# Element-wise work moved from GpSimd to VectorE, and two norms moved behind their products, in a fused convolution, scan, attention and expert kernel

## The chip, the cores and the metric

The kernel runs on one core of a Trainium2 chip. The metric is the time of one execution on the device in microseconds (us). Three timed runs of the kernel before gave 5311.55, 5321.8 and 5326.36 us; the median is 5321.8 us.

A core has TensorE (PE in the profile; PEld is its weight load), VectorE (DVE), ScalarE (ACT), GpSimd (POOL) and SyncE (SP), which here issues the transfers. Each engine works through its own instructions in the order in which the program put them.

## The reference, cut to what matters

The input is four images of 128 channels and 64 x 64 pixels, all float32. Layer 0 is a group norm, then

```
xn  = ln(x);  y = xn + fc2(gelu(ln(conv3x3(xn))))
chunks = ln(y), split in 4 groups of 32 channels
m   = mamba(chunks) + skip * chunks          # scan over the 4096 pixels
out = ln(xn + m) @ proj_w.T + proj_b;  x = x + out
```

In the scan, `delta = softplus(...)`, the state is multiplied by `exp(delta * A)` and driven by `delta * B * xin` (16 states for each of 64 inner channels), and the read-out is gated: `y * silu(z)`. Layer 1 works on the pixels as tokens t:

```
t = t + softmax(q k^T / sqrt(128)) v @ W_proj + b_proj   # q, k, v from ln(t); 4 heads of 32
probs = softmax(ln(t) @ router_w + router_b)             # 8 experts, the best 2, their shares made to sum to 1
t = t + sum over the 2 of share * (ln(t) @ expert_w + expert_b)
```

## The kernel before

The 4096 pixels of an image are 8 blocks of 512 columns (`BLK`). A main loop at the end of the kernel runs in **slots**. Its scan has 512 units (4 images x 8 blocks x 2 halves of the channels x 8 pairs of states) of two slots each, so 1024 slots (`END`). In each slot the loop puts, by hand and in a fixed order, one step of everything on the engines: `tensor`, `vector`, `scalar`, `gpsimd` and `sync` are wrappers (`queued`, L445) that chain each instruction to the previous one of its engine. Nearly all instructions therefore carry line 445, and are told apart by the names of their tiles.

- **Scan.** In a unit ACT makes the decays `da` (`decayed`, L747), DVE multiplies the broadcast rows by `du` (`driven`, L767, tile `h`), runs the scan (`scan`, L772) and multiplies by the read-out rows (`read`, L781, tile `hc`); PE turns and sums `hc` into `y`. ACT also copies the last states (`kept`, L762, tile `state`).
- **Attention.** `attention` (L940) yields one group a slot: 2 tiles of 128 keys against 1024 queries of a head. PE makes the scores `sc`, ACT their exponentials `pT` (`exponentials`, L1001), and PE adds the weighted values into `av` a slot later (`weighted`, L1009). An image has 256 groups. Its keys are taken in 10 runs (`RUNS`, L931) as blocks become ready (`ready`, L936). At the end of a run ACT copies `av` to `avs`, and where an earlier run of the same queries exists (96 of 160), GpSimd adds its sum `prev`.
- **Lanes.** The rest is cut into small steps by `yield`, in two lanes that advance twice a slot each (`advance`, L1186). Lane X does a step at the end of a slot and the next at the start of the following slot; lane Y does its two in the middle. Lane Y: group norm, first norm, `conv` (L611; by PE for the first image, by 9 multiply-adds on DVE for the others) and `inputs` (L681), which prepares a half block for the scan; its softplus correction and `du` are five GpSimd operations (L723 to L727). Lane X: `closed` (L816) ends layer 0 for a block and makes keys, queries and values, and `finished` (L1059) does projection, router and experts. After END lane Y runs `finished` too.
- **Norms.** `normalised` (L504) takes statistics on DVE, a power and a product on GpSimd (`rs`, `shift`), and after two yields four ACT operations (`xt`). In lane X it is used twice in `closed` (on `cm`, then on `tt`) and once in `finished` (on `acc`).
- **`held`** (L532) keeps `inputs` and the first norm of `closed` from using lane X's one PSUM tile at the same time; one waits two steps at a time while the other has it.
- In `finished`, PE also adds the residual: after the expert bias product it multiplies `acc` by the identity into the same PSUM tile, and ACT copies the sum to `res`. Eight expert products follow, with `share` rows fetched from memory.

Of the kernel before, what the change touches and what calls it, by code (L numbers as in the profile page):

```python
# [9 lines left out]
F32 = mybir.dt.float32  # L10
# [7 lines left out]
P = 128  # L18
# [18 lines left out]
def conv_mamba_attn_moe_kernel(ctx: ExitStack, tc: tile.TileContext, t: dict):  # L37
# [65 lines left out]
    with (  # L103
        tc.tile_pool(name="bound", bufs=1) as bd,
        tc.tile_pool(name="ps_w", bufs=2, space=PSUM) as ps_w,
    ):
        pw = ps_w.tile([P, P], F32, name="pw")
        nc.tensor.matmul(pw, lhsT=xdt, rhs=dtT, start=True, stop=True)
        nc.vector.tensor_copy(wdt, pw)
        pw = ps_w.tile([P, P], F32, name="pw")  # L110
        nc.tensor.matmul(pw[0:1, :], lhsT=bvc, rhs=wp, start=True, stop=True)
        crow1 = bd.tile([1, C], F32, name="crow1")
        nc.vector.tensor_add(crow1, pw[0:1, :], bp)
        pw = ps_w.tile([P, P], F32, name="pw")
        nc.tensor.matmul(pw, lhsT=ones, rhs=crow1, start=True, stop=True)
        nc.vector.tensor_copy(crow, pw)

        sq = bd.tile([P, 2 * NH + 1], F32, name="sq")
        nc.vector.memset(sq, 0.0)
        bsq = bd.tile([DH, 2 * NH], F32, name="bsq")
        for i, (w, bias) in enumerate(((wqn, bqn), (wkn, bkn))):
            for h in range(NH):
                r = slice(DH * h, DH * h + DH)
                pw = ps_w.tile([P, P], F32, name="pw")
                nc.tensor.matmul(pw[0:DH, 0:DH], lhsT=w[:, r], rhs=w[:, r], start=True, stop=True)
                g = bd.tile([DH, DH], F32, name="g", bufs=2)
# [24 lines left out]
        nc.gpsimd.memset(power[:, 2 * NH :], 0.5)  # L154
        wn = bd.tile([1, 2 * NH], F32, name="wn")
        nc.gpsimd.tensor_tensor(wn, norm[:, 0 : 2 * NH], power[:, 0 : 2 * NH], ALU.pow)
        nc.gpsimd.tensor_tensor(bnorm, bnorm, power[:, 2 * NH :], ALU.pow)
        most = bd.tile([1, 2 * NH], F32, name="most")
        nc.vector.scalar_tensor_tensor(most, wn, 1.001 * float(C) ** 0.5, bnorm, ALU.mult, ALU.add)
        score = bd.tile([1, NH], F32, name="score")  # L160
        nc.vector.tensor_mul(score, most[:, 0:NH], most[:, NH:])
        fine = bd.tile([1, NH + 1], F32, name="fine")
        nc.vector.tensor_scalar(fine[:, 0:NH], score, SCORE_MAX / ATT_SCALE, None, ALU.is_le)
        nc.vector.tensor_scalar(
            fine[:, NH : NH + 1], norm[:, 2 * NH : 2 * NH + 1], VALUE_MAX, None, ALU.is_le
        )
        ok = bd.tile([1, 1], F32, name="ok")
        nc.vector.tensor_reduce(ok, fine, AX.X, ALU.min)
        nc.vector.tensor_scalar(ok, ok, -1.0, 1.0, ALU.mult, ALU.add)
        nc.vector.tensor_copy(general, ok)  # L170
    setup.close()


# [277 lines left out]
    def mm(out, lhsT, rhs, start=True, stop=True):  # L451
        tensor.matmul(out, lhsT=lhsT, rhs=rhs, start=start, stop=stop)
# [42 lines left out]
    def transposed(lane, src):  # L495
        ps = work(lane)
        for j in range(NT):
            tensor.transpose(ps[:, j * P : (j + 1) * P], src[:, j, :], ident)
        return ps

    def by_tile(src):
        return src.rearrange("p (j c) -> p j c", c=P)

    def normalised(lane, src):  # L504


        st = small.tile([P, NT, 6], F32, name=f"st{lane}")
        mv = small.tile([P, NT, 2], F32, name=f"mv{lane}")
# [3 lines left out]
            vector.bn_aggr(out=mv[:, j, :], in_=st[:, j, :])  # L512
        rs = small.tile([P, NT], F32, name=f"rs{lane}")
        vector.tensor_scalar_add(rs, mv[:, :, 1], EPS)
        shift = small.tile([P, NT], F32, name=f"shift{lane}")
        vector.tensor_scalar_mul(shift, mv[:, :, 0], -1.0)
        gpsimd.tensor_tensor(rs, rs, mhalf, ALU.pow)
# [163 lines left out]
    def inputs(b, i, p):  # L681
# [38 lines left out]

        du = mix.tile([P, BLK], F32, name="du", bufs=2)
        lost = du
        gpsimd.tensor_scalar(lost, e, 1.0, -1.0, ALU.add, ALU.add)  # L723
        gpsimd.tensor_sub(lost, e, lost)
        gpsimd.tensor_add(ln, ln, lost)
        gpsimd.tensor_add(delta, delta, ln)
        gpsimd.tensor_mul(du, delta, xin)  # L727
        in_of[b, i, p] = xin, zs, delta, du, bcd
        done.add(("in", b, i, p))
        yield  # L730
# [55 lines left out]
    def scanned(b, i, p, y):  # L786
        xin, zs, delta, du, bcd = in_of.pop((b, i, p))
        vector.scalar_tensor_tensor(xin, xin, dsk, y, ALU.mult, ALU.add)
        gpsimd.tensor_mul(zs, xin, zs)
        gated[b, i, p] = zs  # L790

    def turned_on(y, term, first, last):
# [23 lines left out]
    def closed(b, i):  # L816
# [23 lines left out]
        done.add(("freed", b, i))  # L840
        yield
        vector.tensor_add(cm, ps, cm)
        gpsimd.tensor_add(by_tile(xr), by_tile(xr), projb[:, None, :].to_broadcast([P, NT, C]))
        yield
        while held:
            yield
            yield
        held.add("closed")
        ps = transposed("X", by_tile(cm))
        yield  # L850
        xt = yield from normalised("X", by_tile(ps))
        held.clear()
        ps = transposed("X", xt)
        yield
        f = tmp("X", "f")
        scalar.activation(f, ps, AF.Identity, bias=lnb, scale=lnw)
        yield
        ps = work("X", [P, NT, C])
        for j in range(NT):
            mm(ps[:, j, :], f[:, j * P : (j + 1) * P], projT)  # L860
        yield
        tt = side.tile([P, NT, C], F32, name="tt")
        vector.tensor_add(tt, ps, by_tile(xr))
        send(tsave[b][:, s], tt.rearrange("p j c -> p (j c)"), 2)
        xt = yield from normalised("X", tt)

        tr = tmp("X", "tr", [P, NT, C])
        gpsimd.tensor_add(tr, tt, crow[:, None, :].to_broadcast([P, NT, C]))
        send(td[:, s], tr.rearrange("p j c -> p (j c)"), 2)
        ps = transposed("X", xt)  # L870
        yield
# [137 lines left out]
    def weighted(group):  # L1009
# [9 lines left out]
                )  # L1019
        if last:  # L1020
            avs = att.tile([P, BLK], F32, name="avs", bufs=2)
            scalar.copy(avs, av)
            if prev is not None:
                gpsimd.tensor_add(avs, avs, prev)


            if not final:
# [31 lines left out]
    def finished(b, qb, lane):  # L1059
# [18 lines left out]
            mm(ps[:, j, :], aT[:, j * P : (j + 1) * P], wp)  # L1078
        yield
        vector.tensor_add(acc, ps, acc)  # L1080
        xt = yield from normalised(lane, acc)
        ps = transposed(lane, xt)
        yield
        xf = tmp(lane, "xf")
        scalar.copy(xf, ps)
# [8 lines left out]

        yield

        pr = routed("pr")
        vector.tensor_add(pr, ps, rb[:, None, :].to_broadcast(wide))
        m = routed("m", 1)
        vector.tensor_reduce(m, pr, AX.X, ALU.max)  # L1100
        vector.tensor_sub(pr, pr, m.to_broadcast(wide))
# [22 lines left out]
        vector.tensor_mul(pr, pr, pick1)  # L1124
        vector.tensor_add(top1, top1, top2)
        vector.reciprocal(top1, top1)
        vector.tensor_mul(pr, pr, top1.to_broadcast(wide))
        yield

        ps = work(lane)  # L1130
        for j in range(NT):
            tensor.transpose(ps[0:NE, j * P : (j + 1) * P], pr[:, j, :], ident)
        yield
        prT = tmp(lane, "prT")[0:NE, :]
        scalar.copy(prT, ps[0:NE, :])
        shares = dram.tile([NE, BLK], F32, name=f"shares{lane}")
        send(shares, prT)
        yield

        def share(e):  # L1140
# [10 lines left out]


        ps = work(lane)
        mm(ps, eb8, prT, True, False)
        for j in range(NT):
            mm(ps[:, j * P : (j + 1) * P], acc[:, j, :], ident, False, j == NT - 1)
        yield
        res = tmp(lane, "res")
        scalar.copy(res, ps)
        yield  # L1160
        ahead = deque(share(e) for e in (0, 2))
        yield
# [106 lines left out]
    units = [(b, i, p, n) for b, i in blocks for p in range(2) for n in range(0, NST, 2)]  # L1269
    END = 2 * len(units)  # L1270

    ALONE = NB // 2 * NST
    rows, due, closing, y_of = {}, deque(), deque(), {}
    h_of, slot = {}, 0

# [182 lines left out]
```

## Time and profile before

| quantity | value |
|---|---|
| median of the timed runs | 5321.8 us |
| profiled execution, its own time | 5310.32 us |
| its span, first to last instruction | 5308.5 us |
| mean granted TensorE clock | 0.956 |
| ACT `pT` / `da` / table loads | 1986.7 / 747.5 / 409.3 us |
| DVE scan `h` x512 | 1256.1 us, 2453 ns each |
| DMA queue 1 | 62.8% of 16 engines' span |

The profile is of one execution. Busy time is what an engine spent inside instructions; idle time of an engine is put down to the instruction that released it. The execution's own time exceeds its span by 1.8 us.

### The profile page before, as it was taken

The page shows a single profiled execution, that of the slowest core. Times are in us where ns is not written, and L with a number is a line of the kernel's source. Part 1 is how long each engine was busy: PE and PEld are TensorE (multiplying, and loading weights), DVE is VectorE, ACT ScalarE, POOL GpSimd, SP SyncE. Part 2 cuts the span into 40 slices and gives each one's busy share as a digit, 9 for nine tenths or more (in the row PEclk, how much of TensorE's full clock was granted, in tenths as well). Part 3 has the DMA queues.
Part 4 walks back from the last instruction along what each step waited for, and adds up shares of the span by engine and source line. Part 5 has one row for each costly group of instructions (what it writes and reads, how often), then busy time and mean ns, then how long its engine had stood idle before and what let it go on. Part 6 is the DMA issues. An engine that isn't in the chain of part 4 may idle for free. (4 is left out here: it accounts for less than half of the span.)

```text
span 5308.5 us, 64113 instructions
## 1 busy us (share of the span) xinstructions
PE 4795.3 (90%) x21066; PEld 2336.3 (44%) x21066; DVE 3691.3 (70%) x5123; ACT 3916.8 (74%) x6117; POOL 1441.9 (27%) x1091
## 2 busy tenths in 40 slices
PE   4556898999999999899999999999999999999997
PEld 2333444444444444444444444444444444443443
DVE  4888767777777877877777877877777877740322
ACT  3455787888888787688888888788888887756553
POOL 2333224333322223223322223323422223201000
PEclk8777999999999999899999999999999999999998
DMA  3555666666766666667766666767766666744532
GB/s 96 182 181 190 211 213 232 234 221 236 250 222 218 237 209 237 223 226 256 252 231 224 230 217 228 262 223 252 250 237 227 227 221 220 261 160 156 178 132 68
DMA packets 451702, 1131.71 MB, mean 213 GB/s; under 512 B 51985, under 2 KB 135330, under 8 KB 451362
## 3 DMA queue, kind: packets, MB, share of 16 engines
q1 hardware_dynamic: 450194, 1126.74, 62.8%
q8 instruction: 169, 2.77, 0.2%
q14 instruction: 171, 1.40, 0.1%
q10 hardware_dynamic: 1168, 0.80, 0.0%
HBM read 967.12 MB, written 143.39 MB: 209 GB/s over the span
## 5 line engine op out<-in xcount | busy, mean ns | idle before, releaser
L445 ACT ACTIVATE pT<-sc 128x1024 f32<-128x1024 f32 x2048 | 1986.7, 1025 | 757.9 <-PE sc L445 755.5
L445 PE MATMUL av<-pT,v 128*64 128x512 f32 x8192 | 1997.8, 609 | 9.0 <-ACT avs L445 8.8
L445 PE MATMUL sc<-qs,ks 128*128 128x512 f32 x4096 | 1305.5, 437 | 96.9 <-DMA ks<-kd 48.3
L445 DVE TENSOR_TENSOR_SCAN h<-da,state,h 128x1025 f32<-128x1025 f32 x512 | 1256.1, 2453 | 131.7 <-ACT h L445 108.1
L445 PEld LDWEIGHTS sc<-qs,ks 128*128 128x128 f32 x4096 | 700.9, 190 | 799.1 <-ACT pT L445 322.6
L445 PEld LDWEIGHTS av<-pT,v 128*64 128x64 f32 x8192 | 499.7, 137 | 838.8 <-issue 808.2
L445 ACT ACTIVATE da<-delta,amat 128x512 f32<-128x512 f32 x1024 | 747.5, 734 | 5.9 <-POOL delta L445 4.0
L445 DVE TENSOR_TENSOR h<-rows,du 128x1024 f32<-128x1024 f32 x512 | 702.7, 1372 | 66.5 <-POOL du L445 25.8
L445 DVE TENSOR_TENSOR hc<-rows,h 128x1024 f32<-128x1024 f32 x512 | 677.3, 1323 | 33.9 <-PE y L445 13.9
L445 PE MATMUL y<-ident,hc 128*128 128x128 f32 x4096 | 622.4, 283 | 64.7 <-DVE hc L445 64.7
L445 PEld LDWEIGHTS y<-ident,hc 128*128 128x128 f32 x4096 | 516.8, 146 | 235.3 <-issue 88.0
L445 POOL TENSOR_TENSOR rsY<-rsY,mhalf 128x4 f32<-128x4 f32 x100 | 148.8, 1488 | 1377.0 <-DVE shiftY L445 1377.0
L445 ACT ACT_TABLE_LOAD x319 | 409.3, 1283 | 22.2 <-PE ps_Y L445 17.1
L445 POOL TENSOR_TENSOR zs<-xin,zs 128x512 f32<-128x512 f32 x64 | 141.3, 2207 | 808.3 <-DVE xin L445 779.6
L445 POOL TENSOR_TENSOR rsX<-rsX,mhalf 128x4 f32<-128x4 f32 x92 | 199.9, 2172 | 537.8 <-DVE shiftX L445 537.4
L445 POOL TENSOR_TENSOR avs<-avs,prev 128x512 f32<-128x512 f32 x96 | 152.4, 1588 | 642.4 <-ACT avs L445 556.9
L445 ACT ACTIVATE xt<-ps_Y,shiftY,rsY 128x128 f32<-128x128 f32 x380 | 143.6, 469 | 112.7 <-POOL shiftY L445 105.7
L445 PE MATMUL ps_X<-share,w_ew 128*128 128x512 f32 x432 | 214.4, 619 | 0.0
L445 POOL TENSOR_SCALAR du<-e 128x512 f32<-128x512 f32 x64 | 127.5, 1992 | 289.0 <-ACT e L445 289.0
L445 DVE TENSOR_TENSOR share<-share,xf 128x1024 f32<-128x1024 f32 x128 | 156.8, 1225 | 47.7 <-DMA share<-sharesY 32.0
L445 DVE RECIPROCAL den<-den 128x32 f32<-128x32 f32 x16 | 5.5, 346 | 220.0 <-DMA den<-total 219.9
L445 ACT COPY avs<-av 128x512 f32<-128x512 f32 x160 | 95.2, 595 | 81.2 <-PE av L445 66.2
(238 smaller groups left out, 4394.2 us busy)
## 6 DMA issues: line engine op xcount, KB each, us to landing
rows<-bcd SPq DMA_DIRECT2D x1024, 512.0 KB
ks<-kd SPq DMA_DIRECT2D x192, 512.0 KB
qs<-qd SPq DMA_DIRECT2D x161, 512.0 KB
share<-sharesX SPq DMA_DIRECT2D x108, 512.0 KB
v<-vd SPq DMA_DIRECT2D x192, 256.0 KB
ks<-kd SPq DMA_DIRECT2D x128, 256.0 KB
avd<-avs SPq DMA_DIRECT2D x96, 256.0 KB
prev<-avd SPq DMA_DIRECT2D x96, 256.0 KB
```

Of the source, the lines that this page charges most:

```text
L445: return lambda *args, **kw: queued(op(*args, **kw))
```

## The change

**GpSimd to VectorE.** The five softplus operations of `inputs`, the gate product in `scanned` (L786), the two row additions in `closed` (`projb` into `xr`, `crow` into `tr`) and the addition of `prev` at the end of an attention run are issued on DVE. The last reads `av` from PSUM itself, so ACT copies `av` only where there is no `prev`. GpSimd keeps the powers (and the small products and copies beside them).

**Norms behind products.** The mean is taken out of the weights: at the start, `rw`, each expert's matrix and `projT` (with `lnw` in it, and `lnb` folded into `projb`) are multiplied by `ident - 1/128` (`centred`). In `closed` the first norm gives way to `spread` (statistics and power only): `cm` is multiplied by `projT` as it is, and `rs` multiplies the product as it is added to `xr`. In `finished` the raw `acc` is turned, `rs` multiplies the router's logits, and a second copy of the shares, multiplied by `rs`, goes to the experts. The residual is added by DVE from the turned `acc` (`xf`), not by PE. `closed` has four yields fewer and no longer looks at `held`; `finished` has two fewer. The second norm of `closed` and the norms of lane Y stay.

```diff
+        cen = bd.tile([P, P], F32, name="cen")
+        nc.vector.tensor_scalar(cen, ident, 1.0 / C, None, ALU.subtract)
+        def centred(w, src):
+            n = w.shape[1]
+            for k in range(0, n, P):
+                pw = ps_w.tile([P, P], F32, name="pw")
+                m = min(P, n - k)
+                nc.tensor.matmul(pw[:, 0:m], lhsT=cen, rhs=src[:, k : k + m], start=True, stop=True)
+                nc.vector.tensor_copy(w[:, k : k + m], pw[:, 0:m])
+        centred(rw, rw)
...
+        centred(ewf, ewf)
...
+        centred(projT, gain)
...
+    def spread(lane, src):
+        mv, rs = moments(lane, src)
+        gpsimd.tensor_tensor(rs, rs, mhalf, ALU.pow)
+        return rs
...
-        gpsimd.tensor_scalar(lost, e, 1.0, -1.0, ALU.add, ALU.add)
-        gpsimd.tensor_sub(lost, e, lost)
-        gpsimd.tensor_add(ln, ln, lost)
-        gpsimd.tensor_add(delta, delta, ln)
-        gpsimd.tensor_mul(du, delta, xin)
+        vector.tensor_scalar(lost, e, 1.0, -1.0, ALU.add, ALU.add)
+        vector.tensor_sub(lost, e, lost)
+        vector.tensor_add(ln, ln, lost)
+        vector.tensor_add(delta, delta, ln)
+        vector.tensor_mul(du, delta, xin)
...
-        gpsimd.tensor_mul(zs, xin, zs)
+        vector.tensor_mul(zs, xin, zs)
...
-        while held:
-            yield
-            yield
-        held.add("closed")
         ps = transposed("X", by_tile(cm))
         yield
-        xt = yield from normalised("X", by_tile(ps))
-        held.clear()
-        ps = transposed("X", xt)
-        yield
-        f = tmp("X", "f")
-        scalar.activation(f, ps, AF.Identity, bias=lnb, scale=lnw)
+        rs = spread("X", by_tile(ps))
         yield
         ps = work("X", [P, NT, C])
         for j in range(NT):
-            mm(ps[:, j, :], f[:, j * P : (j + 1) * P], projT)
+            mm(ps[:, j, :], cm[:, j * P : (j + 1) * P], projT)
         yield
         tt = side.tile([P, NT, C], F32, name="tt")
-        vector.tensor_add(tt, ps, by_tile(xr))
+        for j in range(NT):
+            vector.scalar_tensor_tensor(
+                tt[:, j, :], ps[:, j, :], rs[:, j : j + 1], xr[:, j * P : (j + 1) * P],
+                ALU.mult, ALU.add,
+            )
...
-            scalar.copy(avs, av)
-            if prev is not None:
-                gpsimd.tensor_add(avs, avs, prev)
+            if prev is None:
+                scalar.copy(avs, av)
+            else:
+                vector.tensor_add(avs, av, prev)
...
-        xt = yield from normalised(lane, acc)
-        ps = transposed(lane, xt)
+        rs = spread(lane, acc)
+        yield
+        ps = transposed(lane, acc)
...
-        vector.tensor_add(pr, ps, rb[:, None, :].to_broadcast(wide))
+        vector.tensor_mul(pr, ps, rs[:, :, None].to_broadcast(wide))
+        vector.tensor_add(pr, pr, rb[:, None, :].to_broadcast(wide))
...
-        vector.tensor_mul(pr, pr, top1.to_broadcast(wide))
+        vector.tensor_mul(both[:, :, 0:NE], pr, top1.to_broadcast(wide))
+        vector.tensor_mul(both[:, :, NE:], both[:, :, 0:NE], rs[:, :, None].to_broadcast(wide))
...
-        mm(ps, eb8, prT, True, False)
-        for j in range(NT):
-            mm(ps[:, j * P : (j + 1) * P], acc[:, j, :], ident, False, j == NT - 1)
+        mm(ps, eb8, prT[0:NE, :])
         yield
         res = tmp(lane, "res")
-        scalar.copy(res, ps)
+        vector.tensor_add(res, ps, xf)
```

More of the change, by code (lines that the diff above doesn't have):

```diff
@@ L170, in conv_mamba_attn_moe_kernel @@
         nc.vector.tensor_copy(general, ok)
+        cen = bd.tile([P, P], F32, name="cen")
[8 more added lines that the diff above has]
+        centred(rw, rw)
+        ewf = ew.rearrange("p e c -> p (e c)")
+        centred(ewf, ewf)
+        gain = bd.tile([P, C], F32, name="gain")
+        nc.vector.tensor_scalar_mul(gain, projT, lnw)
+        pw = ps_w.tile([P, P], F32, name="pw")
+        lnbs = bd.tile([P, P], F32, name="lnbs")
+        nc.vector.tensor_copy(lnbs, lnb.to_broadcast([P, P]))
+        nc.tensor.matmul(pw, lhsT=lnbs, rhs=projT, start=True, stop=True)
+        nc.vector.tensor_add(projb, pw, projb)
+        centred(projT, gain)
     setup.close()
@@ L502, in by_tile, with moments @@
         return src.rearrange("p (j c) -> p j c", c=P)
-    def normalised(lane, src):
+    def moments(lane, src):
         st = small.tile([P, NT, 6], F32, name=f"st{lane}")
@@ L514, in normalised @@
         vector.tensor_scalar_add(rs, mv[:, :, 1], EPS)
+        return mv, rs
+    def spread(lane, src):
+        mv, rs = moments(lane, src)
+        gpsimd.tensor_tensor(rs, rs, mhalf, ALU.pow)
+        return rs
+    def normalised(lane, src):
+        mv, rs = moments(lane, src)
         shift = small.tile([P, NT], F32, name=f"shift{lane}")
@@ L842, in closed @@
         vector.tensor_add(cm, ps, cm)
-        gpsimd.tensor_add(by_tile(xr), by_tile(xr), projb[:, None, :].to_broadcast([P, NT, C]))
+        vector.tensor_add(by_tile(xr), by_tile(xr), projb[:, None, :].to_broadcast([P, NT, C]))
         yield
-        while held:
-            yield
-            yield
-        held.add("closed")
         ps = transposed("X", by_tile(cm))
         yield
-        xt = yield from normalised("X", by_tile(ps))
-        held.clear()
-        ps = transposed("X", xt)
-        yield
-        f = tmp("X", "f")
-        scalar.activation(f, ps, AF.Identity, bias=lnb, scale=lnw)
+        rs = spread("X", by_tile(ps))
         yield
@@ L867, in closed @@
         tr = tmp("X", "tr", [P, NT, C])
-        gpsimd.tensor_add(tr, tt, crow[:, None, :].to_broadcast([P, NT, C]))
+        vector.tensor_add(tr, tt, crow[:, None, :].to_broadcast([P, NT, C]))
         send(td[:, s], tr.rearrange("p j c -> p (j c)"), 2)
@@ L1095, in finished @@
         yield
+        both = routed("both", 2 * NE)
         pr = routed("pr")
-        vector.tensor_add(pr, ps, rb[:, None, :].to_broadcast(wide))
+        vector.tensor_mul(pr, ps, rs[:, :, None].to_broadcast(wide))
+        vector.tensor_add(pr, pr, rb[:, None, :].to_broadcast(wide))
         m = routed("m", 1)
@@ L1131, in finished @@
         for j in range(NT):
-            tensor.transpose(ps[0:NE, j * P : (j + 1) * P], pr[:, j, :], ident)
+            tensor.transpose(ps[0 : 2 * NE, j * P : (j + 1) * P], both[:, j, :], ident)
         yield
-        prT = tmp(lane, "prT")[0:NE, :]
-        scalar.copy(prT, ps[0:NE, :])
+        prT = tmp(lane, "prT")[0 : 2 * NE, :]
+        scalar.copy(prT, ps[0 : 2 * NE, :])
         shares = dram.tile([NE, BLK], F32, name=f"shares{lane}")
-        send(shares, prT)
+        send(shares, prT[NE:, :])
         yield
@@ L1270, in conv_mamba_attn_moe_kernel @@
     END = 2 * len(units)
-    ALONE = NB // 2 * NST
     rows, due, closing, y_of = {}, deque(), deque(), {}
```

## The prediction

> **What bounds the kernel now.** I first read the page's busy shares, then the table by stage, cut where the stages change: setup, the scan alone (no or few attention groups), scan and attention together, attention after the last scan, and the chain at the end.
>
> ```profile
> PE 4795.3 (90%) x21066; PEld 2336.3 (44%) x21066; DVE 3691.3 (70%) x5123; ACT 3916.8 (74%) x6117; POOL 1441.9 (27%) x1091
> ```
>
> ```profile
> 0.00:98.00 98.00, 39.68 (x113) 19.21 (x114) 23.71 (x127) 23.13 (x38) 17.63 (x44) 0.86 0.25 72
> 98.00:600.00 502.00, 313.71 (x1234) 174.05 (x1232) 407.35 (x436) 290.84 (x538) 171.65 (x116) 0.77 0.55 185
> 600.00:4675.00 4075.00, 3849.26 (x17358) 1886.85 (x17360) 3111.96 (x4138) 3263.64 (x5129) 1212.70 (x890) 0.98 0.69 232
> 4675.00:5200.00 525.00, 518.01 (x2116) 222.35 (x2112) 120.92 (x345) 308.48 (x374) 37.52 (x39) 1.00 0.44 148
> 5200.00:5308.50 108.50, 74.68 (x249) 33.82 (x248) 27.34 (x79) 30.69 (x41) 2.41 (x4) 0.76 0.20 65
> ```
>
> The columns are the stretch, its length, busy time of PE, PEld, DVE, ACT and POOL, granted clock, DMA share and GB/s. From 600 to 5200 us PE is busy for 4367 of 4600 us, 95%, and at 99% busy its clock is still 1.00. Here the time is PE's work plus 226 us (3849 of 4075) and 7 us of idle time. From 98 to 600 us it isn't PE: DVE is busy 81%, PE 62%. So GpSimd is nowhere the bound, and what counts is PE work removed, PE idle time, and DVE's first 600 us. Next, the waits of PE from 600 to 4675 us (us in total, times, longest):
>
> ```profile
> PE sc L445 <- ACT pT L445: 41.6, 117, 2.6
> PE sc L445 <- DMA ks<-kd: 35.1, 15, 6.8
> PE ps_Y L445 <- ACT xt L445: 26.3, 21, 2.5
> PE ps_X L445 <- ACT xa L445: 23.4, 15, 2.5
> PE ps_X L445 <- ACT xt L445: 22.6, 10, 8.4
> ...
> PE y L445 <- DVE hc L445: 10.5, 7, 3.8
> ```
>
> ACT ends half of it; DVE's `hc` only 10.5 us. Last, the groups of instructions by form, of the whole run:
>
> ```profile
> L445 POOL TENSOR_TENSOR avs<-avs,prev 128x512 f32<-128x512 f32 x96 | 152.4, 1588 | 642.4 <-ACT avs L445 556.9 <-DMA rows<-bcd 42.5 <-DMA prev<-avd 16.0
> L445 DVE TENSOR_TENSOR aT<-aT,inv 128x512 f32<-128x512 f32 x32 | 22.8, 721 | 67.3 <-DMA inv<-inverse 48.9 <-issue 10.6 <-DMA rows<-bcd 4.7
> L445 DVE TENSOR_TENSOR res<-res,ps_X 128x512 f32<-128x512 f32 x108 | 74.2, 687 | 108.8 <-PE ps_X L445 108.0
> L445 PE MATMUL ps_X<-ident,xt 128*128 128x128 f32 x368 | 70.0, 308 | 64.9 <-ACT xt L445 63.1 <-ACT bc L445 1.1
> L445 PE MATMUL ps_X<-ident,acc 128*128 128x128 f32 x216 | 32.2, 293 | 0.0
> ```
>
> The same kind of addition costs 1588 ns on POOL and 690 on DVE. For PE I use busy time divided by count (70.0/368 = 190 ns), since the 308 ns overlap with the next matmul.
>
> **What the Trainium skill says.** "Perfetto Trace Analysis", section Identifying the Most-Contended Engine, warns that matmul busy share is a poor measure of distance from the roofline. I use it only for whether PE stands still, and the timeline agrees: at 2613.05 us `av` runs for 1.94 us, `sc` follows at 2614.91, a lane product at 2615.95, the next at 2617.76, `av` again at 2618.81, with no gap. "GPSIMD Engine Reference", section Engine selection, has GpSimd about 2 times slower for two inputs; here 1588 against 690 ns, 2.3 times. "SBUF — State Buffer", section Who interferes with whom: a DVE instruction with two SBUF inputs, or in a two-port mode, locks with a GpSimd instruction that reads SBUF, and one with a single SBUF input does not. The trace agrees: `hc` (two SBUF inputs) has median 1219 and maximum 2305 ns, while `res` + PSUM stays within 679 and 689 ns.
>
> **Part 1, GpSimd's operations on DVE.** Added on DVE: softplus, one tensor_scalar (0.54 us, the undisturbed `gn`; 1.08 under the lock) and four two-input operations (0.69, the median of `aT`), 3.3 us x 64 = 211; gate 0.69 x 64 = 44; `avs` from PSUM 0.69 x 96 = 66; row additions 0.69 x 64 = 44. Together 365 us. Taken off DVE: waiting for the lock. Means less medians: `driven` 152 ns x 512 = 78, `hc` 103 x 512 = 53, scan 100 x 512 = 51, the smaller groups (taps, `cm` with skip, `gn`) 31; 213 us. The moved operations and the dropped `shift` products are 1010 of POOL's 1442 us, 70%, so I take 149 us (bounds 0 and 213). Off ACT: 96 copies of `avs` x 0.595 = 57 us.
>
> What this does to the end: in the PE-bound stage DVE has 963 us idle, of which 850 are waits for PE's lane products, so the work lands in waits. Cover fails where work comes in a lump: softplus is issued late in a slot of lane Y and stands before the next unit's `h`, scan and `hc`. The lump is 3.3 us less some 1.5 us of lock (213 of 1240 us of POOL's 512-column work and powers is 17%; 8.6 us of chain x 17%), 1.8 us net. A `hc` is wanted by PE a slot after its issue (4075 us for 444 scans of two slots is 4.6 us), so I expect little: +15 us of PE waits, from 0 to 64 x 1.8 = 115. DVE's new wait for `av` has behind it the next slot's `h` and lane X's step; PE has scores (1.2 us) and `y` (0.6) to do before it needs `av` again, which covers 0.69. I take 0 (bounds -8, the present `av<-avs` wait, and 96 x 0.69 = 66). SP's sends of `avs`, `tt` and `tr` wait for shorter work than now, and none is moved behind a longer one: 0.
>
> In the stage of 98 to 600 us DVE is nearest the bound. Added: 9 softplus and 8 gates = 35 us, row additions 5. Less lock: `h`, `hc` and scan 31 x 0.7, with `cm` and `gn` some 25. So +15 us of work. But ACT waits there for `shift` (36 us in lane Y's norms) behind the POOL chains, DVE waits 25.8 us for the first `du` (8.5 us of it the POOL chain, 3.3 on DVE), and 24.5 for ACT. I take -25 for these, and -10 net (bounds +20 and -35).
>
> **Part 2, norms behind products.** PE: `closed` loses four transposes a block, 32 x 4 x 0.19 = 24 us; `finished` loses the `acc` products, 32.2 in lane X and 6.7 in lane Y = 39. Of these 63 us, 45 lie between 600 and 4675 us (28 blocks x 4 x 0.177 = 19.8, and 25.5) and 14 after it. All of that is path: **-45 and -14**. Turning `acc` replaces turning `xt`, and 16 rows of shares replace 8 in the same matmuls: 0.
>
> ACT loses `xt` of `closed` (128 x 0.38 = 49), of `finished` (52), `f` (27) and the copy of `res` (19); with `avs` 204 us. DVE gains 4 x 0.28 - 0.69 = 0.43 us x 32 for the product times `rs` (the 128-column price is that of the statistics on PSUM), 0.38 x 32 for the router, 0.69 x 32 for the residual, less 64 x 0.16 of `shift`: 38 us, beside PE's work. DVE's sum is 3691 + 365 + 38 - 149 = 3945 us.
>
> PE's idle time: `ps_X<-xt` loses two of three users (-14), `sc<-pT` I halve, since ACT has 204 us less to do and fewer `xt` that wait for POOL (86 us of such waits in the stage) in front of `pT` (-20); `ps_Y<-xt` loses 10 as the powers no longer queue behind POOL's chains; +15 from part 1. **-30** (bounds -100, and +40 if the lumps hurt more).
>
> **Slots.** `closed` loses four steps, two slots, so block 2 frees attention two slots earlier. Two groups (3 us each, the pure attention slots at the end) move into the stage where PE has room: **-6** (0 to -15). **End.** In the last chain a power, its product and four `xt` (2.9 us) and POOL's part of a sum go; `acc` products there mostly lie beside share transfers: **-6** (0 to -12). **Start.** The centring adds 11 products and some 14 DVE operations of 0.29 us, in a stretch where DVE and PE alternate: **+5** (2 to 12); it also waits for the expert weights.
>
> Sum: -45 - 14 - 30 - 10 - 6 - 6 + 5 = -106 us. On the profiled execution's own 5310.3 that is 5204; the median of the runs is 11.5 above that execution, so 5216 against 5321.8, or -2.0%. The bounds of the terms taken together run from about 5110 to 5330.
>
> **Rivals.** *The coupling between ACT, POOL and PE is worth more*: 410 us of table loads and the waits for POOL make ACT late in lumps, and with 204 us less work most ACT-ended waits of PE go. Then idle falls by 90 rather than 30 and the first 600 us by 35: 5216 - 60 - 25 = 5131, say 5110 to 5165. For it: ACT ends half of PE's waits. Against: ACT itself waits 542 us for scores in that stage, so it is usually early. Chance 0.24.
> *VectorE becomes late.* One mechanism: the softplus lump in front of `h`, scan and `hc`; PE then waits for `hc`, and ACT, behind its copy of `state`, for the scan. From 98 to 600 us, with DVE at 81%, PE waits for `hc` 54 us already; after the change DVE is at about 83% in the main stage. If 2.7 us of the 3.3 are uncovered, 64 x 2.7 = 173 against the +15 in my sum: 5216 + 158 = 5374. It decides from 1.9 us uncovered on (121 us, the other terms' gain). Chance 0.10.
> *It doesn't do what it says*: PE's place is taken by waits (`ks` transfers at a DMA share of 0.69, `xa`), and the removed 59 us come back as idle: 5306 to 5338. Chance 0.06.
>
> **Numbers.** Forecast 5216, chance 0.60, its own range 5165 to 5300. A measurement of this kernel can tell about 0.3% from no change. The range leaves out the slow rival, half of the no-change case and the far side of the fast one: 5115 to 5310. Faster 0.84, same 0.06, slower 0.10.
>
> **What would show it.** PE busy falls by about 63 us to 4730; POOL's to some 430; ACT's by 204 and DVE's rises by about 250; maximum `hc` 2.3 us becomes rare and its mean nears 1219 ns; PE's idle from 600 us on shrinks by tens of us; the first attention group comes two slots earlier. I would be wrong if PE's wait for `hc`, or ACT's for the scan, grew beyond 100 us, or if `av` waited for DVE's `avs`.

## The result, and the profile after

The changed kernel takes 5238.1 us (median of four runs, 5221.2 to 5238.8) against 5322.6 us of the kernel before (a fourth run has joined the three of above): a ratio of 0.984, interval 0.982 to 0.986. It is 84 us faster; 106 were forecast. The profiled execution of the changed kernel is the lowest of its four, 5221.2 us with a span of 5219.4, so the two profiles differ by 89 us. Each stage is read from where its first and last scan begins:

| stage | before, us | after, us | difference | forecast |
|---|---|---|---|---|
| start to the first scan | 99.9 | 99.4 | -0.5 | +5 |
| first to 68th scan | 495.8 | 482.5 | -13 | -10 |
| 68th to the last scan | 4076.5 | 4024.0 | -52.5 | -75 |
| last scan to the end | 636.3 | 613.5 | -23 | -26 |

The busy line of the page after:

```profile
PE 4743.5 (91%) x20704; PEld 2300.7 (44%) x20704; DVE 3834.5 (73%) x5809; ACT 3749.8 (72%) x5701; POOL 423.5 (8%) x483
```

DVE was to rise by 254 us and rose by 143. The table by stage, with the prediction's columns:

```profile
0.00:98.00 98.00, 42.27 (x132) 23.06 (x133) 29.79 (x146) 22.70 (x37) 11.28 (x40) 0.87 0.22 62
98.00:600.00 502.00, 327.90 (x1262) 182.68 (x1261) 423.19 (x535) 292.81 (x543) 58.15 (x57) 0.77 0.57 192
600.00:4606.00 4006.00, 3803.11 (x17057) 1851.63 (x17056) 3209.72 (x4665) 3129.99 (x4785) 341.50 (x373) 0.98 0.70 236
4606.00:5110.00 504.00, 496.70 (x2004) 210.96 (x2004) 142.70 (x383) 274.42 (x304) 10.60 (x11) 0.99 0.45 151
5110.00:5219.40 109.40, 73.52 (x256) 32.37 (x252) 29.09 (x83) 29.91 (x35) 2.02 (x2) 0.79 0.23 75
```

From 600 us to the last scan PE is still busy 95% (3803 of 4006 us), and idle for 203 us. The waits of PE in that stretch (us in total, times, longest) have other names than before:

```profile
PE ps_X L467 <- DVE bothX L467: 40.7, 21, 4.0
PE sc L467 <- ACT pT L467: 28.0, 86, 1.6
PE sc L467 <- DMA ks<-kd: 24.1, 12, 4.7
PE ps_X L467 <- DVE lo L467: 20.3, 23, 2.7
PE ps_Y L467 <- ACT xt L467: 15.7, 9, 6.2
PE y L467 <- DVE hc L467: 13.2, 5, 6.7
```

ACT's `xt` and `xa` in lane X are gone from the top. In their place stand DVE's `bothX`, the router's last tile, and `lo`. Last, the groups by form that answer to those shown of before:

```profile
L467 DVE TENSOR_TENSOR res<-res,ps_X 128x512 f32<-128x512 f32 x108 | 73.7, 682 | 51.9 <-PE ps_X L467 51.5
...
L467 DVE TENSOR_TENSOR avs<-av,prev 128x512 f32<-128x512 f32 x96 | 66.1, 689 | 252.9 <-PE av L467 238.3 <-DMA total<-avs 5.4 <-DMA rows<-bcd 5.2
...
L467 PE MATMUL ps_X<-ident,xt 128*128 128x128 f32 x132 | 27.8, 320 | 7.1 <-ACT xt L467 6.8
...
L467 DVE TENSOR_TENSOR aT<-aT,inv 128x512 f32<-128x512 f32 x32 | 21.8, 689 | 64.1 <-DMA inv<-inverse 58.9 <-issue 5.2
...
L467 PE MATMUL ps_X<-ident,acc 128*128 128x128 f32 x108 | 18.2, 292 | 0.0
```

The turns of `xt` in lane X fell from 70.0 to 27.8 us and the `acc` products from 32.2 to 18.2; what is left of `acc` is its turning, now in place of that of `xt`. `avs` costs 0.689 us as taken. DVE now waits 238 us for `av`; run 3 tests what that costs. The sign of being wrong that the prediction named is the other way about, PE's `av` waiting for DVE's `avs`: that is 12.4 us, where PE waited 8.8 us for ACT's `avs` before. Two groups of the scan, from the page after:

```profile
L467 DVE TENSOR_TENSOR_SCAN h<-da,state,h 128x1025 f32<-128x1025 f32 x512 | 1204.2, 2352 | 90.0 <-ACT h L467 56.2
...
L467 DVE TENSOR_TENSOR hc<-rows,h 128x1024 f32<-128x1024 f32 x512 | 624.2, 1219 | 16.1 <-PE y L467 5.9
```

The scan's mean was 2453 ns and is 2352; `hc` has a mean of 1219 ns, the median that it had before. So in these groups all of VectorE's waits beside GpSimd have gone, not 70% of them.

### The profile page after: what moved, and what is told of

Read it like the earlier page. It is cut to its first block, busy times and chain, and to the rows that moved or that the text cites. A ratio compares the mean times of both kernels' runs of the same rounds, so it can differ in the third digit from the quotient of the medians.

```text
span 5219.4 us, 62693 instructions
## 1 busy us (share of the span) xinstructions
PE 4743.5 (91%) x20704; PEld 2300.7 (44%) x20704; DVE 3834.5 (73%) x5809; ACT 3749.8 (72%) x5701; POOL 423.5 (8%) x483
## 4 chain that ended last, share of the span: by engine, by line
PE 55%; DVE 18%; ACT 13%; DMA 6%; issue 5%; POOL 2%; SPq 1%; DVEq 0%; ACTq 0%; POOLq 0%
PE av L467 23%; PE sc L467 13%; PE ps_X L467 8%; DVE h L467 6%; PE ps_Y L467 5%; PE y L467 5%; ACT pT L467 4%; ACT L467 3%; DMA ks<-kd 2%; DVE hc L467 2%; ACT xt L467 1%; ACT e L467 1%; DMA rows<-bcd 1%; DVE stX L467 1%; POOL rsX L467 1%
## 5 line engine op out<-in xcount | busy, mean ns | idle before, releaser
L467 PE MATMUL av<-pT,v 128*64 128x512 f32 x8192 | 1998.3, 609 | 12.4 <-DVE avs L467 12.4
L467 PE MATMUL sc<-qs,ks 128*128 128x512 f32 x4096 | 1296.1, 436 | 64.4 <-DMA ks<-kd 32.7
L467 DVE TENSOR_TENSOR_SCAN h<-da,state,h 128x1025 f32<-128x1025 f32 x512 | 1204.2, 2352 | 90.0 <-ACT h L467 56.2
L467 PE MATMUL y<-ident,hc 128*128 128x128 f32 x4096 | 626.6, 284 | 64.9 <-DVE hc L467 64.9
L467 DVE TENSOR_TENSOR hc<-rows,h 128x1024 f32<-128x1024 f32 x512 | 624.2, 1219 | 16.1 <-PE y L467 5.9
L467 DVE TENSOR_TENSOR h<-rows,du 128x1024 f32<-128x1024 f32 x512 | 623.4, 1218 | 14.2 <-DMA rows<-bcd 13.7
L467 POOL TENSOR_TENSOR rsX<-rsX,mhalf 128x4 f32<-128x4 f32 x92 | 203.8, 2216 | 2524.6 <-DVE rsX L467 2440.5
L467 POOL TENSOR_TENSOR rsY<-rsY,mhalf 128x4 f32<-128x4 f32 x100 | 130.4, 1304 | 2071.0 <-DVE shiftY L467 1560.3
L467 DVE TENSOR_TENSOR avs<-av,prev 128x512 f32<-128x512 f32 x96 | 66.1, 689 | 252.9 <-PE av L467 238.3
L467 ACT COPY state<-h 128x2 f32<-128x2 f32 x448 | 88.7, 198 | 93.5 <-DVE h L467 93.5
L467 DVE SCALAR_TENSOR_TENSOR cm<-y,w_fc1w,cm 128x512 f32<-128x512 f32 x192 | 142.8, 744 | 3.4
L467 PE MATMUL ps_Y<-pairs,inxc 128*128 128x512 f32 x256 | 129.2, 629 | 15.6 <-DMA pairs<-xn 10.3
L467 PEld LDWEIGHTS ps_X<-share,w_ew 128*128 128x128 f32 x432 | 73.6, 190 | 146.8 <-issue 98.5
```

Source lines behind the costliest of these rows:

```text
L467: return lambda *args, **kw: queued(op(*args, **kw))
```

## The experiments

Times are medians of four runs, and ratios, with a 95% interval, are those to runs of the kernel before made beside them, unless said otherwise. "After" is the changed kernel, 5238 us, 0.984.

**1 and 2. One part of the change alone.** The first keeps the norms where they were, the second keeps GpSimd's operations where they were. The edits are the two halves of the change as described above.

> Part 1 alone: the kernel before, with GpSimd's operations on 512 columns on VectorE, norms as before. My theory (the gain is TensorE work taken away plus waits of TensorE for ScalarE that go, less new waits for VectorE, which now stands in order behind the end of each attention run): no TensorE work goes here, so 5300 to 5335 us, ratio 0.996 to 1.003, while the means of h, hc and scan fall to 1219, 1219 and 2353 ns. Rival (the gain comes from the shared-port waits that VectorE loses, 217 us): ratio 0.985 to 0.990.

> Part 2 alone: norms behind products, residual added by VectorE, GpSimd keeps its operations on 512 columns. My theory: TensorE's busy time falls by about 52 us as in the changed kernel, ScalarE's by about 147, and there is no wait of VectorE for av: 5215 to 5255 us, ratio 0.980 to 0.987, as fast as the changed kernel or faster. Rival (the shared port): VectorE keeps its means of 1370 and 1320 ns, ratio 0.992 to 0.996.

Part 1 alone took 5290.6 us, 0.993 (0.991 to 0.996): 30 us less than the 5320.4 of before beside it, more than my theory gave it and less than the rival did. It takes no work from PE (4799.5 us busy against 4795.3); PE's waits fell from 505 to 484 us. Part 2 alone took 5279.8 us, 0.992 (0.989 to 0.994): 41 us, less than my theory gave it, and at the edge of what the rival did. There PE is busy for 33 us less, and PE's waits sum to 507 us: no less than before. Yet those that ACT ends fell from 264 to 153. The waits of PE in part 2 alone, whole run:

```profile
...
PE y L467 <- DVE hc L467: 60.7, 22, 8.9
PE ps_X L467 <- DVE bothX L467: 59.7, 26, 6.3
PE ps_Y L467 <- DVE gn L467: 54.7, 25, 9.8
```

The waits that DVE ends grew by 111 us, as much as ACT's lost. Most of that, 84 us, is in `bothX`, at the end of the router's chain (59.7 us, where its forerunner `prX` had 12.6), and in `gn`, the group norm of the next block (54.7 against 18.1). They come with part 2, and not with the work that part 1 puts on DVE.

**3. The sums of attention runs back on ACT and GpSimd.**

```diff
-            if prev is None:
-                scalar.copy(avs, av)
-            else:
-                vector.tensor_add(avs, av, prev)
+            scalar.copy(avs, av)
+            if prev is not None:
+                gpsimd.tensor_add(avs, avs, prev)
```

> The changed kernel with the sums of attention runs as before (ScalarE copies av, GpSimd adds prev). My theory: VectorE's 238 us of waits for av go, TensorE's waits that VectorE ends (bothX 46, stX 24, gn 37, lo 20) fall by about half, and the time falls to 5195 to 5225 us, ratio 0.976 to 0.982. Rival (VectorE had the time to wait, and ScalarE gets 57 us back and VectorE some 25 us of port waits): 5238 to 5260 us, ratio 0.984 to 0.988.

5240.4 us, 0.984 (0.982 to 0.986), the same as after, and PE's waits sum to 468 us in both. So VectorE's 238 us of waiting for `av` don't show in the time. The run trades them for 50 us more of ACT's busy time and 171 of GpSimd's, with 20 less of VectorE's, and it can't tell whether two small effects cancel.

**4. The softplus operations and `du` back on GpSimd** (the five lines of the diff undone).

> The changed kernel with the five softplus operations back on GpSimd. My theory (the lump of 3.2 us on VectorE costs little, as TensorE's wait for hc is 65 us before and after): VectorE loses 204 us of work and gets some 80 us of port waits back; 5230 to 5255 us, within 0.3% of the changed kernel, ratio 0.982 to 0.988. Rival (the lump makes VectorE late): 5190 to 5220 us, ratio 0.975 to 0.981, with TensorE's waits for bothX, stX and gn down by half.

5255.7 us, 0.987 (0.985 to 0.989), 18 us slower than after; the runs (5250.5 to 5262.0) don't overlap those of after. Moving the lump to VectorE thus gains. What changes in the profile is the time of VectorE's two-input operations, as in the group of `hc` in this run:

```profile
L467 DVE TENSOR_TENSOR hc<-rows,h 128x1024 f32<-128x1024 f32 x512 | 659.2, 1288 | 19.3 <-PE y L467 7.9 <-DVE h L467 0.9
```

1288 ns, where after has 1219. VectorE lost 204 us of work and its busy time fell from 3834.5 to 3811.5 us only: 181 us came back as waits beside GpSimd. PE's waits rose by 16 us, most of all for `gn` (37.2 to 57.9). That the chain of five takes longer on GpSimd is not what costs: VectorE waits 25.5 us in all for its `du` here, and 26.9 us for ACT's `e` ahead of its own chain after.

**5, 6 and 7. Steps put back.** After experiment 2 I held that the shorter lanes of part 2 bring PE to products whose inputs DVE hasn't finished. Run 5 puts two empty steps between the router's chain and the turning of `both`. Run 6 gives `closed` and `finished` their lost steps back. Run 7 does so for `finished` alone.

```diff
 # 5
         vector.tensor_mul(both[:, :, NE:], both[:, :, 0:NE], rs[:, :, None].to_broadcast(wide))
         yield
+        yield
+        yield
 # 6; 7 has only the first two
         rs = spread(lane, acc)
         yield
+        yield
+        yield
...
         rs = spread("X", by_tile(ps))
         yield
+        yield
+        yield
+        yield
+        yield
```

> The changed kernel with two more steps (one slot) between VectorE's chain for the router and the transposes of its result. My theory (the new waits of TensorE for VectorE come from lane X's shorter timetable and are time on the path): TensorE's wait for bothX falls from 46 us to under 5 and the time by about as much, 5190 to 5215 us, ratio 0.975 to 0.980. Rival (the idle time only moves to another wait, as TensorE is caught by VectorE's lateness wherever they meet next): 5228 to 5248 us, ratio 0.982 to 0.986.

> The changed kernel with the same work, but with the steps that it dropped put back empty: four in closed, two in finished. My theory (timetable): TensorE's waits that VectorE ends fall from 269 us to 190 or less, nearer to the 163 of before; attention starts two slots later (+6 us); 5175 to 5220 us, ratio 0.973 to 0.981. Rival (VectorE's longer chains are the cause, not the timetable): the waits stay above 240 us, 5238 to 5260 us, ratio 0.984 to 0.988.

> The changed kernel with only the two empty steps of finished put back. They move the router's chain by one slot, from the slot after one with h and scan (3.6 us of VectorE) to the slot after one with hc alone (1.2 us). My theory: the wait for bothX falls from 46 to about 13 us, as prX before; 5200 to 5225 us, ratio 0.977 to 0.982. Rival (the waits stem from the steps that closed dropped, or from longer chains): bothX stays above 35 us, ratio 0.983 to 0.987.

They took 5240.8 us, 0.985 (0.983 to 0.986); 5236.0 us, 0.984 (0.982 to 0.986); and 5246.7 us, 0.986 (0.984 to 0.987). None gains. In run 7 `bothX` fell to 12.8 us, as my theory had it, and the time didn't fall. The waits of PE in run 5, whole run:

```profile
PE y L467 <- DVE hc L467: 94.7, 55, 9.0
...
PE sc L467 <- DMA ks<-kd: 43.4, 22, 6.7
```

`bothX`, 45.9 us of the whole run after, is down to 2.5, and in its place `hc` rose from 64.9 to 94.7 and `ks` from 32.7 to 43.4. In run 6 the waits that DVE ends fell from 269 to 200, as the theory of the lost steps has it, but ACT's rose from 142 to 190 and DMA's from 57 to 86. So that theory names the releaser rightly and not the time.

**8. The residual on PE again.**

```diff
-        mm(ps, eb8, prT[0:NE, :])
+        mm(ps, eb8, prT[0:NE, :], True, False)
+        for j in range(NT):
+            mm(ps[:, j * P : (j + 1) * P], acc[:, j, :], ident, False, j == NT - 1)
...
-        vector.tensor_add(res, ps, xf)
+        scalar.copy(res, ps)
```

> The changed kernel with the residual added by TensorE again (256 products of acc with the identity, 39 us of TensorE's time) and ScalarE's copy in place of VectorE's addition. My theory (work on TensorE is path after 600 us): TensorE's busy time rises by 39 us and the time by 25 to 45, 5263 to 5283 us, ratio 0.988 to 0.993. Rival (TensorE's work is hidden by other waits, so that only part 1 pays): 5238 to 5250 us, ratio 0.983 to 0.987.

5255.9 us, 0.987 (0.986 to 0.989): 18 us. The groups of PE's `acc` products grew by 38.7 us (18.2 to 50.2 in lane X, 3.5 to 10.2 in lane Y). PE's busy time is 4782.0 us, 39 more than after and 15 to 35 more than in the other profiles with the same products (4747.0 to 4766.6). So this work costs less than its groups show, about half by the medians. That is a rough figure: by the two intervals the 18 us are uncertain by some 14, and the run also trades 22 us of VectorE's additions for 19 us of ACT's copies, which it can't tell from the products.

**9 and 10. ACT's work in the preparation of a half block.** On the timeline after, PE's idle time lies close to these ACT steps. At 2580 us, for one (start, duration, engine, operation):

```profile
2580.93 0.69 ACT L467 ACTIVATE e<-ps_Y,w_dtb 128x512 f32<-128x512 f32 x1
2581.65 0.63 ACT L467 ACTIVATE e<-e 128x512 f32<-128x512 f32 x1
2582.30 1.28 ACT L467 ACT_TABLE_LOAD   x1
2583.59 0.63 ACT L467 ACTIVATE ln<-e 128x512 f32<-128x512 f32 x1
2584.13 0.67 ACT L467 ACTIVATE delta<-ps_Y,w_dtb 128x512 f32<-128x512 f32 x1
2584.82 1.28 ACT L467 ACT_TABLE_LOAD   x1
```

These are 5.2 us in a row without a `pT` or a `da`. Over 54 such places between 620 and 4550 us, in steps of 5 us about the start of `e`, ACT is busy 98% in the 10 us that follow and DVE only 51% and 37% in the two steps up to +5; from +5 to +20 DVE is busy 91 to 93%, and PE, which was at 94 to 100% in the four steps up to +5, is at 85 to 95% until +25. So I held that this lump sets PE's idle time. Run 9 takes two operations out of it, on to DVE; run 10 makes it longer.

```diff
 # 9
-        scalar.copy(bc, pb[0:DI, :])
+        vector.tensor_copy(bc, pb[0:DI, :])
...
-        scalar.activation(delta, ps, AF.Relu, bias=dtb)
+        vector.tensor_scalar(delta, ps, dtb, 0.0, ALU.add, ALU.max)
 # 10
         scalar.copy(bc, pb[0:DI, :])
+        scalar.copy(bc, pb[0:DI, :])
+        scalar.copy(bc, pb[0:DI, :])
+        scalar.copy(bc, pb[0:DI, :])
```

> The changed kernel with two operations of each half block's preparation moved from ScalarE to VectorE: the copy bc and the relu that makes delta (1.24 us of ScalarE, 64 times). In the 15 us around these steps ScalarE is 98% busy, VectorE 27 to 50%, and in the 20 us after them VectorE is over 90% busy and TensorE waits. Theory (this lump of ScalarE sets TensorE's idle time, whatever wait it is put down to): idle time falls by 30 to 70 us, 5170 to 5210 us, ratio 0.972 to 0.979. Rival (VectorE's own work sets it): VectorE has 88 us more, 5240 to 5275 us, ratio 0.985 to 0.991.

> The changed kernel with the copy bc done four times instead of once (1.7 us more of ScalarE in the same steps, 64 times, 109 us in all). Theory (the lump of ScalarE is on the path): 50 to 110 us slower than the changed kernel, 5288 to 5348 us, ratio 0.993 to 1.005. Rival (ScalarE, which waits 938 us for scores, takes it in): at most 5250 us, ratio under 0.987.

Run 9 took 5235.5 us, 0.983 (0.981 to 0.985): no change, which neither theory had. ACT's busy sum fell from 3749.8 to 3688.1 us and DVE's rose from 3834.5 to 3923.4. Run 10 took 5286.8 us, 0.994 (0.992 to 0.995): 49 us for 111 us of copies, a little under what the theory gave. PE's wait for the exponentials, 30.5 us of the whole run after, is in run 10:

```profile
PE sc L467 <- ACT pT L467: 101.7, 143, 3.4
```

A longer lump on ACT does reach PE, and costs under half of its size. A shorter one whose work goes to DVE doesn't help. No run relieved ACT and DVE at once, so what fixes the idle time that is left stays open.

**11 and 12. GpSimd's time beside VectorE: the port or the queue.** Both add 537.7 us of GpSimd work to the changed kernel, after the softplus of each half block, with a result that nothing uses. Run 11 reads SBUF, run 12 only writes it. The shared port of the expectations is the lock of the prediction, between a two-input VectorE instruction and a GpSimd instruction that reads SBUF.

```diff
-        bc = tmp("Y", "bc")[0:DI, :]
+        whole = tmp("Y", "bc")
+        bc, aside = whole[0:DI, :], whole[DI:, :]
...
 # 11
+        fixed = taps[DI:, 0:NT, :].rearrange("p k c -> p (k c)")
+        for _ in range(5):
+            gpsimd.tensor_add(aside, fixed, fixed)
 # 12
+        for _ in range(16):
+            gpsimd.memset(aside, 0.0)
```

> The changed kernel with five additions of 512 columns added on GpSimd at the place where softplus stood, on constants and on 64 partitions, whose result nobody uses. Theory (part 1 pays through the shared port: a GpSimd instruction that reads SBUF holds up VectorE's two-input ones): h, hc and scan lose some 80 us together, 15 to 30 us slower than the changed kernel, 5253 to 5268 us, ratio 0.987 to 0.991. Rival (part 1 pays through GpSimd's queue, in which the powers stood behind these operations): as slow as the next run, which only fills the queue.

> The changed kernel with sixteen memsets of 512 columns added on GpSimd at the same place: about 8.5 us of its queue, as the five softplus operations took, but nothing read from SBUF. Theory (shared port): h, hc and scan keep 1219, 1219 and 2353 ns; within 10 us of the changed kernel, 5230 to 5248 us, ratio 0.982 to 0.986. Rival (queue): the powers come late, ScalarE waits 50 us or more longer for shiftY and shiftX, 5253 to 5275 us, ratio 0.987 to 0.991.

Run 11 took 5321.6 us (12 runs, 5317.7 to 5333.2), 0.999 (0.998 to 1.000). It loses all that the change had gained, 84 us, where I expected 15 to 30. Run 12 took 5233.0 us, 0.983 (0.982 to 0.985), no different from after. The groups by form of run 11:

```profile
L467 DVE TENSOR_TENSOR_SCAN h<-da,state,h 128x1025 f32<-128x1025 f32 x512 | 1234.5, 2411 | 84.3 <-ACT h L467 50.8 <-DVE h L467 0.5
...
L467 DVE TENSOR_TENSOR hc<-rows,h 128x1024 f32<-128x1024 f32 x512 | 652.6, 1275 | 14.4 <-PE y L467 4.1 <-DVE h L467 0.4
...
L467 POOL TENSOR_TENSOR bc<-taps 64x512 f32<-64x512 f32 x320 | 537.7, 1681 | 24.7 <-POOL shiftX L467 0.2
```

and of run 12:

```profile
L467 DVE TENSOR_TENSOR_SCAN h<-da,state,h 128x1025 f32<-128x1025 f32 x512 | 1204.6, 2353 | 92.4 <-ACT h L467 59.4
...
L467 POOL MEMSET bc<- 64x512 f32 x1024 | 537.7, 526 | 58.9 <-POOL xn L467 0.3 <-POOL shiftX L467 0.2
```

The scan is 2411 ns beside the adds and 2353 beside the memsets, `hc` 1275 and 1220. VectorE's busy sum grew by 174 us in run 11 and by 3.5 in run 12. The two also differ in the number and length of the instructions, five long ones against sixteen short ones.

PE itself was slower in run 11: a granted clock of 0.947 against 0.958 after and 0.956 in run 12, and `av` busy 2025 against 1998 us. By the profiles, PE's busy sum is 48 us above after and its waits 52 us (520 against 468), so longer waits are only about half of what the two differ by. The trace shows where the other half comes in. One place of run 11's timeline of PE:

```profile
4006.64 1.94 PE L467 MATMUL av<-pT,v 128*64 128x512 f32 x8
...
4013.26 1.12 PE L467 MATMUL ps_Y<-ident,gn 128*128 128x128 f32 x4 [3.56 <-DVE gn L467]
...
4015.16 3.68 PE L467 MATMUL av<-pT,v 128*64 128x512 f32 x8
...
4020.46 1.94 PE L467 MATMUL av<-pT,v 128*64 128x512 f32 x8
```

PE waits 3.56 us for a late `gn`, the granted clock is at half from 4012.2 to 4019.0 us, and the same eight products take 3.68 us in place of 1.94. Between the 68th and the last scan PE stands still for more than 3 us 29 times in run 11, and 10 times after. The clock is at half in 39 stretches that begin there, 222 us in all, against 21 and 123 us after, and in both traces each of these stretches begins in or within 6 us of a standstill of at least 1.4 us. So a long wait of PE costs its own length and then slower products. That the wait causes the slow clock is inferred from this order; no run sets the clock by itself.

## Why the prediction was right, and where it was off

The forecast of 5216 us lay 22 us below the 5238 measured. The direction was right, and so was what the change does: PE loses work, ACT ends fewer of its waits, and VectorE's waits beside GpSimd go. What was mis-sized lies mostly in the main stage, -52.5 us against -75.

Two of the other stages came out near the forecast, with terms that were off and made up for each other. In the first 600 us (-13 against -10) VectorE's work grew by 3 us and not 15, and its idle time fell by 16 and not 25. In the last stage (-23 against -26) PE's work fell by 25 us, more than the 20 of the products and the moved groups, and its idle time rose by 2 where the end was to give 6. The start (-0.5 against +5) lies outside its bounds of 2 to 12: PE and VectorE have 3 and 6 us more to do there, and it takes no longer. PE's wait for `hc` stayed at 65 us, where 15 more were forecast and none was the lower bound. The first attention group came earlier: its `pT` starts at 368.1 us instead of 385.0, and block 1's `vd`, which opens it, is sent after the 39th scan where it was after the 40th. That is the two slots of the step "Slots".

**"All of that is path"**, the term for PE's work, was too large. Between the same two scans, the 68th and the last, the profiles before and after have (columns as in the table by stage):

```profile
595.70:4672.20 4076.50, 3846.47 (x17344) 1885.19 (x17344) 3113.54 (x4138) 3261.18 (x5126) 1216.92 (x892) 0.98 0.69 232
581.90:4605.90 4024.00, 3814.22 (x17096) 1858.94 (x17096) 3226.69 (x4699) 3137.51 (x4804) 350.04 (x381) 0.98 0.70 236
```

So PE lost 32 us of work, with 45 forecast, and 20 us of idle time (230 to 210), with 30 forecast. The products that went had the size forecast: by group, `xt` in lane X and `acc` shrink by 45 us in this stage, and over the whole run by 63 (the turns of `xt` by 42.2 in lane X and 3.8 in lane Y, `acc` by 14.0 and 3.2). Two things took some of that back. First, some 5 us of attention came into this stage (`av` x6784 before, x6808 after). The prediction had it go where PE has room, but the first 600 us have as many as they had (x192). Second, neighbouring instructions overlap in the profile, so that groups count some time twice: PE's groups sum to 5283 us before, and PE is busy for 4795. A group that goes takes less from the busy time than it shows. ACT has the same: its groups shrank by the 204 us forecast, its busy time by 167.

**PE's idle time**, forecast as -30 with ACT's waits as its source, has two thirds of the size forecast and another account. The waits of PE of the whole run by the engine that ends them, in us (the sums hold up to 3 us that no engine ends):

| kernel | ACT | DVE | DMA | sum |
|---|---|---|---|---|
| before | 264 | 163 | 78 | 505 |
| part 1 alone | 229 | 169 | 83 | 484 |
| part 2 alone | 153 | 274 | 79 | 507 |
| both (after) | 142 | 269 | 57 | 468 |
| after, steps put back (run 6) | 190 | 200 | 86 | 479 |
| after, share step later (run 5) | 143 | 261 | 68 | 473 |

ACT's waits fell by 122 us, far more than I gave them: the rival of the coupling was right in that most of the waits that ACT ended in the main stage would go. But DVE's grew by 107. In the main stage alone ACT's fell by 84, DVE's grew by 80, where I had taken 15, and DMA's fell by 14. The runs with steps put back shift the waits between ACT, DVE and DMA and leave the sum at 473 to 479, no lower than after. The prediction took each wait as if it could be removed by itself. Here it couldn't: when waits were taken away, others grew by most of it. Nor were the two parts redundant: they gave 30 and 41 us alone and 84 together, so within the intervals (about 12 us each) they add or do slightly better.

**VectorE's sum** was forecast as 3945 us and is 3834.5. Of these 110 us, 68 are waits beside GpSimd: all of the 217 us went and I had taken 149 (`h` 79, `hc` 53, scan 52, the taps, `cm` with skip and `gn` 33). Some 24 are overlap again: VectorE's groups grew by 168 us together, its busy time by 143. I had given the third of the waits that stayed to the powers that GpSimd keeps. They don't hold VectorE up: after the change 79 of the `h`, `hc` and scan instructions start while a power runs, and the longest `hc` of all is 1.23 us. It is the powers that get longer. In lane X the 84 powers that overlap one of these instructions take 2.33 us on average, and the other 8 take 1.01. One reading was wrong too: of VectorE's waits from 600 to 4675 us, put at 850 us for PE's lane products, PE ends 656.

The section Who interferes with whom of "SBUF — State Buffer" in the Trainium skill has a two-input VectorE instruction contend with a GpSimd instruction that reads SBUF, and not with one that only writes it. Runs 11 and 12 agree: 538 us of GpSimd's additions add 174 us to VectorE's time, and as much time of memsets adds 3.5. The powers read SBUF as well, and there the delay falls on GpSimd.

So the lock is shown to cost this kernel time (runs 4 and 11), and GpSimd's filled queue is shown not to (run 12). That part 1's gain is the lock's is the best account, and not proven for all of it: part 1 alone also shortens ACT's work. ACT's waits for `shift`, behind the powers in GpSimd's queue, were 207 us before and are 215 with part 1 alone, so they are not where it gained. The clock may have a share too: the two profiles, at clocks of 0.956 before and 0.955 with part 1 alone, differ by 17 us and the medians by 30, and the 29 runs of before made beside the experiments had clocks of 0.948 to 0.956, those of part 1 alone 0.955 to 0.957.

The five softplus operations on VectorE were feared as a lump. They are nearly free in its busy sum, since their 204 us stand in place of 181 us of waits (run 4).

**The rivals.** "VectorE becomes late" is refuted in the form it had, the softplus lump ahead of `hc`: PE's wait for `hc` was 64.7 us and is 64.9, and run 4 finds that the lump gains on VectorE. VectorE did become late for others of PE's products, `bothX`, `gn` and `lo` above all. "It doesn't do what it says" described one half of the truth: work and waits that are removed return in part, but not in whole.

**What stays open** is what sets the 210 us of PE's idle time in the main stage. About half of it, 114 us, lies in the 25 us from the start of `e` of each half block, which are a third of the stage. Lengthening ACT's part of that makes the kernel slower (run 10), but relieving ACT at DVE's cost doesn't make it faster (run 9). I found no version that is faster than the changed kernel by more than the intervals.

## What to carry to other kernels

Before a wait is booked as gain, ask what is late next: read the sum of the bound engine's waits, and not the one that carries a name, and take the size of removed work from the engine's busy time, not from the sum of its groups: here 45 us of groups in the main stage were 32 us of it. A long operation of GpSimd that reads SBUF (512 columns here) costs VectorE time in its two-input operations, so moving it to VectorE can add much less than its duration. Change parts one at a time on the chip: here the part without any work taken from TensorE gave over a third of the gain.

## What the runs showed of the hardware

- GpSimd's additions of 64 x 512 elements in SBUF (1681 ns each, 320 of them) cost the kernel 84 us; memsets that took just as long (526 ns, 1024 of them) cost nothing.
- In run 11 a standstill of PE of 3.56 us is followed by a half clock, and the same eight products take 3.68 us in place of 1.94. In the main stage the clock is at half for 222 us in run 11, with 29 standstills over 3 us, and for 123 us after, with 10.
- The power on 128 x 4 elements takes 2216 ns a piece in lane X and 1304 in lane Y after. None of the 79 `h`, `hc` and scan instructions that start while one runs is longer than 1.23 us (`h`, `hc`) or 2.36 us (scan), as they are without one.
